# Summing attention scores in three bursts of matmuls a chunk instead of seven

## The chip, the cores and the metric

The kernel runs on one core of a Trainium2 chip. The metric is the device time of one execution in microseconds (us), the median of several runs. The engines are named as in the profile: PE is TensorE (matmuls, with PEld for its weight loads), DVE is VectorE, ACT is ScalarE, POOL is GpSimd, and SP issues most of the transfers.

## The reference

The input is a float32 image batch of 16 x 56 x 56 pixels with 384 channels. Two residual layers are applied:

```python
x = x + attention(group_norm(x))          # layer 0
x = x + binary_depthwise_conv(group_norm(x))   # layer 1, 3x3
```

Layer 0 projects every pixel to a query, a key and a value (384 -> 3 x 384). The channels fall into three groups of 128, which use neighbourhoods of 3 x 3 pixels at distances (dilations) of 1, 2 and 3 pixels. Each group has four heads of 32 channels. For each pixel and head,

```python
score[k] = sum over 32 channels of q[c] * key[c at neighbour k]   # k = 0..8
a = softmax(score / sqrt(32))
out[c] = sum over k of a[k] * value[c at neighbour k]
```

and the result goes through a 384 -> 384 projection with a bias. The change is about the first of these lines: three groups times nine neighbours are 27 "taps", and for each tap four sums over 32 channels are wanted at every pixel.

## The kernel before, in words

An image is cut into seven chunks of eight rows, 448 pixels, so there are 112 chunks. Channels lie on the 128 partitions and pixels along the free dimension. Three plans describe the work on one chunk: `plan_a` turns the input to channels-first and gathers statistics, `plan_b` does attention, `plan_c` does the second layer. Each plan places its pieces at a step and an order within the step with `at(step, order, piece)`. A chunk follows the one before it by nine steps (`STEP = 9`), so work of many chunks is interleaved: in the nine steps in which chunk m forms its scores, the values of earlier chunks are weighed, the keys of a later chunk are projected, and still older chunks are convolved. At the end all pieces are issued by step and order; within a step scores come before convolutions, those before the weighing, queries, key and value projections, output projections, and the turning of inputs and outputs. The framework fixes each engine's instruction order when the kernel is built, near this order but not the same, and gives out the buffers of the pools; on the chip every engine works through its own list.

The score work of a chunk, steps 0 to 8:

- `query(g)` (L435) fills the one PSUM buffer `pq` with the query of group g: six matmul records of L416. It is placed at step -1 + 3g, that is one step before the products of its group.
- `score(i)` (L458), i = 0 to 8, is one row of three taps: one DVE multiplication (L466) of `pq` with three shifted views of the key gives a tile `t` of 128 x 1344. Tiles come from the pool `t_p`.
- `score_round()` (L441) sums taps over the channels of each head. For one tap this is a matmul of the tap's 448 columns with a constant `sel` of 128 x 32 (L451), which adds up four heads and puts them into four of 32 rows of `ps`. Tap p goes to rows 32(p mod 4) onward, so four taps in a row use four different column quarters of PE and can run side by side. Call four such taps a round; 27 taps make seven rounds, the last one of three.
- Every float32 matmul shows as two records, so a full round is 8 MATMUL records.
- Before, a round is issued as soon as four taps are ready: after i = 1, 2, 3, 5, 6, 7 and 8. That makes seven bursts. `in_one_go` keeps a burst together, and puts the newest tap first, so that the one wait for DVE is at the start.
- After the last round `softmax_1` copies `ps` out and the weights are formed.

Other PE work that is named below: `pkv` is the projection of keys and values (L416, 12 records for one key and one value group, at steps 0, 3 and 6), `po` the output projection (L562, 6 records, steps 6, 7 and 8), `pb_a` the spreading of softmax weights over channels (L529, each step), `pc` the second layer's convolution (L656, 24 records, steps 2 and 5, with 32 output columns as in a score round), `pt_x`, `pt_o` and `pt_s` transpositions.

`xr` (pool `xr_p`) holds the residual of a chunk, three tiles of 128 x 448, the same size as one `t`. `load_residual` fetches it, `out_project` adds to it (L565), and after the third part it is stored to `x1d` (L570), which frees it.

Of the kernel before, what the change touches and what calls it, by code (L numbers as in the profile page):

```python
# [20 lines left out]
NG = 3  # L21
NTAP = 9
NQ = 4
# [12 lines left out]
def dilated_attention_then_binary_conv(  # L36
# [186 lines left out]

    dr_p = ctx.enter_context(tc.tile_pool(name="dr_p", bufs=3, space=DRAM))
    xn_p = ctx.enter_context(tc.tile_pool(name="xn_p", bufs=3))
    xr_p = ctx.enter_context(tc.tile_pool(name="xr_p", bufs=2))
    t_p = ctx.enter_context(tc.tile_pool(name="t_p", bufs=3))
    w_p = ctx.enter_context(tc.tile_pool(name="w_p", bufs=3))
    y_p = ctx.enter_context(tc.tile_pool(name="y_p", bufs=4))
    s_p = ctx.enter_context(tc.tile_pool(name="s_p", bufs=1))  # L230
# [30 lines left out]
    def rows(ap):  # L261
        return ap.rearrange("p (r w) -> p r w", w=W)

    def three(t, d, ky):

        tw = t[:, ky * d : ky * d + ROWS, 0:W]
        return bass.AP(tw.tensor, tw.offset, [tw.ap[0], (d, 3), *tw.ap[1:]])

    def in_one_go(matmuls):

        matmuls[0]()
        with tc.high_priority():
            for m in matmuls[1:]:
                tc.keep_in_program_order(m())
# [126 lines left out]
    def plan_b(m, t0):  # L401
# [36 lines left out]

        ready = []

        def score_round():  # L441

            burst = ready[:NQ]
            del ready[:NQ]
            if "ps" not in had:
                had["ps"] = ps_s.tile([P, 512], F32, tag="s", name="ps")

            def add(p, tk):
                j, i = p % NQ, p // NQ
                s0 = SEL0 - 4 * i  # L450
                return nc.tensor.matmul(  # L451
                    had["ps"][32 * j : 32 * j + 32, :PX], sel[:, s0 : s0 + 32], tk,
                    start=(i == 0), stop=(p + NQ >= NG * NTAP),
                )

            in_one_go([lambda a=a: add(*a) for a in burst[-1:] + burst[:-1]])

        def score(i):  # L458

            g, ky = divmod(i, 3)  # L460
            d = DIL[g]
            qg = rows(had["q"][:, :PX])
            q3 = bass.AP(qg.tensor, qg.offset, [qg.ap[0], (0, 3), *qg.ap[1:]])
            k3 = three(kv[0][g][m % K_SLOTS], d, ky)
            t = t_p.tile([P, 3, PX], F32, tag="t", name="t")
            nc.vector.tensor_tensor(t.rearrange("p k (r w) -> p k r w", w=W), q3, k3, ALU.mult)  # L466
            ready.extend((i * 3 + kx, t[:, kx, :]) for kx in range(3))
            if len(ready) >= NQ or i == 8:
                score_round()

        GH = NG * HEADS
        weights = ew.rearrange("p (s v) -> p s v", s=NSUB)[:, :, :NR]
# [121 lines left out]
        for i in range(9):  # L594
            at(t0 + i, SCORE, lambda i=i: score(i))
# [188 lines left out]
```

## Time and profile before

| | before |
|---|---|
| median of 3 runs | 5464.58 us (5464.06 to 5466.99) |
| profiled span | 5462.3 us |
| PE busy | 5293.4 us (97%) |
| POOL busy | 4212.5 us (77%) |
| DVE busy | 4157.7 us (76%) |
| ACT busy | 2412.6 us (44%) |
| score matmuls `ps` L451 | 6048 records, 751.9 us busy |

"Busy" is the time in which an engine has at least one instruction in flight. Matmuls are pipelined, so PE can be busy all the time and still lose time between two kinds of matmul; such losses are read from the starts of consecutive groups in the timeline. A time in the timeline is the start of a group of like instructions, followed by how long the group was in flight.

### The profile page before, as it was taken

How to read it: one execution, taken by the hardware profiler on the slowest of the kernel's cores; microseconds unless marked ns; L12 is line 12 of the kernel's file. 1: busy time of each engine (PE TensorE's matmuls, PEld its weight loads, DVE VectorE, ACT ScalarE, POOL GpSimd, SP SyncE). 2: the span in 40 equal slices, each digit the busy share in tenths (PEclk: the TensorE clock that was granted, in tenths of full speed). 3: DMA queues.
4: the chain of work that ended last, by engine and by line, in shares of the span. 5: the costliest groups of instructions: out<-in, count | busy, mean ns of one | idle time of the engine just before them, and what ended most of it. 6: DMA issues, size and time to landing. Idle time of an engine off the chain costs nothing. (4 is left out here: it accounts for less than half of the span.)

```text
span 5462.3 us, 76025 instructions
## 1 busy us (share of the span) xinstructions
PE 5293.4 (97%) x26901; PEld 2335.4 (43%) x26901; DVE 4157.7 (76%) x4179; ACT 2412.6 (44%) x4203; POOL 4212.5 (77%) x3041
## 2 busy tenths in 40 slices
PE   6999999999999999999999999999999999999956
PEld 4443444444444444444444444444444444444422
DVE  3887778777777777777777778777777777877843
ACT  2223444444444444444444444544444444444433
POOL 1667788788888888888888888888888888888860
PEclk8999999999999999999999999999999999999975
DMA  5433556555555555555555555555555555545435
GB/s 165 131 105 107 153 159 166 159 156 156 157 159 160 158 159 164 155 158 158 160 164 155 160 160 159 162 158 158 155 157 157 161 161 159 160 133 135 129 93 140
DMA packets 833859, 827.88 MB, mean 152 GB/s; under 512 B 381379, under 2 KB 823238, under 8 KB 833478
## 3 DMA queue, kind: packets, MB, share of 16 engines
q1 hardware_dynamic: 825280, 817.58, 55.0%
q10 hardware_dynamic: 8198, 5.43, 0.3%
q8 instruction: 213, 3.49, 0.3%
q14 instruction: 168, 1.38, 0.1%
HBM read 468.47 MB, written 231.21 MB: 128 GB/s over the span
## 5 line engine op out<-in xcount | busy, mean ns | idle before, releaser
L544 POOL TENSOR_TENSOR w<-w 128x1344 f32<-128x1344 f32 x672 | 2049.9, 3050 | 516.2 <-DVE w L536 493.1
L466 DVE TENSOR_TENSOR t<-pq,k 128x1344 f32<-128x1344 f32 x1008 | 1535.6, 1550 | 247.7 <-PE pq L416 244.6
L416 PE MATMUL pkv<-xn,wqkvT 128*128 128x448 f32 x4032 | 1671.1, 554 | 1.3 <-ACT xa L382 1.2
L536 DVE TENSOR_TENSOR w<-pb_a,v 128x1344 f32<-128x1344 f32 x1008 | 1557.3, 1545 | 141.0 <-PE pb_a L529 74.7
L416 PEld LDWEIGHTS pkv<-xn,wqkvT 128*128 128x128 f32 x4032 | 719.9, 190 | 773.6 <-issue 727.5
L562 PE MATMUL po<-y,wprojT 128*128 128x448 f32 x2016 | 839.1, 551 | 36.1 <-POOL y L548 36.1
L416 PE MATMUL pq<-xn,wqkvT 128*128 128x448 f32 x2016 | 852.5, 558 | 0.0
L709 POOL TENSOR_TENSOR m<-m 128x1344 f32<-128x1344 f32 x210 | 639.3, 3044 | 216.0 <-ACT m L703 215.9
L639 ACT ACTIVATE z<-z,mrz 96x448 f32<-96x448 f32 x896 | 617.1, 751 | 361.4 <-DMA z<-x1d 310.9
L451 PE MATMUL ps<-t,sel 128*32 128x448 f32 x6048 | 751.9, 552 | 6.0 <-DVE t L466 6.0
L703 ACT ACTIVATE m<-zg,ktap 128x448 f32<-128x448 f32 x945 | 556.2, 657 | 292.0 <-POOL m L709 287.6
L656 PE MATMUL pc<-z,kdiag 96*32 96x440 f32 (+1 forms) x5376 | 578.5, 565 | 46.1 <-ACT z L639 26.7
L562 PEld LDWEIGHTS po<-y,wprojT 128*128 128x128 f32 x2016 | 375.2, 191 | 398.3 <-issue 345.0
L565 DVE SCALAR_TENSOR_TENSOR xr<-po,bias,xr 128x448 f32<-128x448 f32 x336 | 228.6, 680 | 369.3 <-PE po L562 369.2
L416 PEld LDWEIGHTS pq<-xn,wqkvT 128*128 128x128 f32 x2016 | 355.0, 190 | 328.9 <-issue 328.9
L663 DVE TENSOR_TENSOR x<-pc,x 128x448 f32<-128x448 f32 x224 | 139.8, 624 | 386.9 <-PE pc L656 386.9
L548 POOL TENSOR_TENSOR y<-y,w 128x448 f32<-128x448 f32 x336 | 382.5, 1138 | 23.4
L529 PE MATMUL pb_a<-aT,spread 24*128 24x448 bf16 x3024 | 383.3, 359 | 11.5 <-DVE w L536 11.2
L547 POOL TENSOR_TENSOR y<-w 128x448 f32<-128x448 f32 x336 | 382.3, 1138 | 13.8
L426 ACT COPY v<-pkv 128x448 f32<-128x448 f32 x336 | 179.6, 535 | 446.6 <-PE pkv L416 436.9
L382 ACT COPY xa<-pt_x 128x448 f32<-128x448 f32 x336 | 179.0, 533 | 399.3 <-PE pt_x L378 376.8
L426 ACT COPY k<-pkv 128x448 f32<-128x448 f32 x336 | 179.1, 533 | 391.9 <-PE pkv L416 391.3
(113 smaller groups left out, 4146.8 us busy)
## 6 DMA issues: line engine op xcount, KB each, us to landing
z<-x1d SPq DMA_DIRECT2D x608, 224.0 KB, 4.4
xn<-xd SPq DMA_DIRECT2D x112, 672.0 KB, 4.6
xr<-xd SPq DMA_DIRECT2D x112, 672.0 KB, 4.3
x1d<-xr SPq DMA_DIRECT2D x112, 672.0 KB, 3.2
out_dram<-osb SPq DMA_DIRECT2D x448, 168.0 KB, 2.9
xin<-in_x_dram SPq DMA_DIRECT2D x108, 672.0 KB, 7.0
xd<-xa SPq DMA_DIRECT2D x315, 224.0 KB, 3.1
x<-x1d SPq DMA_DIRECT2D x112, 448.0 KB, 8.2
```

The lines of the kernel that those rows point to most:

```text
L416: nc.tensor.matmul(dst[:, :PX], wqkvT[:, cc, o0 : o0 + P], had["xn"][:, cc, :], start=(cc == 0), stop=(cc == NG - 1))
L451: return nc.tensor.matmul(had["ps"][32 * j : 32 * j + 32, :PX], sel[:, s0 : s0 + 32], tk, start=(i == 0), stop=(p + NQ >= NG * NTAP),)
L466: nc.vector.tensor_tensor(t.rearrange("p k (r w) -> p k r w", w=W), q3, k3, ALU.mult)
L529: return nc.tensor.matmul(pb[:, kx, :PX].rearrange("p (s n) -> p s n", s=NSUB), spread[rows_of, v % 2, :], had["a"][rows_of, :, v // 8, :] ...
L536: nc.vector.tensor_tensor(w.rearrange("p k (r w) -> p k r w", w=W), pb[:, :, :PX].rearrange("p k (r w) -> p k r w", w=W), three(kv[1][g][m ...
L544: nc.gpsimd.tensor_tensor(w0, w0, w, ALU.add)
L548: nc.gpsimd.tensor_tensor(y, y, w0[:, 2], ALU.add)
L562: nc.tensor.matmul(po[:, :PX], wprojT[:, g, j * P : (j + 1) * P], had[f"y{g}"], start=(g == 0), stop=(g == NG - 1))
L639: nc.scalar.activation(z[:, q], z[:, q], AF.Identity, bias=mrz[:, j, q, 0:1], scale=mrz[:, j, q, 1:2])
L656: return nc.tensor.matmul(pcr[q * HD : (q + 1) * HD, :, lo:hi], kdiag[:, kx, j * NQ + q, :], rows(z[:, q])[:, :, lo + kx - 1 : hi + kx - 1 ...
L703: nc.scalar.activation(rows(t[:, kx]), zp[:, ky : ky + ROWS, kx : kx + W], AF.Copy, scale=ktap[:, o : o + 1])
L709: nc.gpsimd.tensor_tensor(had["m"], had["m"], t, ALU.add)
```

## The change

The rounds are gathered into three bursts, after i = 2, 5 and 8, of two, two and three rounds (8, 8 and 11 matmuls). The aim is to have fewer changes between the score matmuls and other PE work. Up to four tiles `t` are alive then: after i = 2 one of nine taps is left over, and after i = 5 two of ten. So `t_p` gets four buffers instead of three, and the memory comes from `xr_p`, which goes from two to one. The flags that start and stop a sum in `ps` are counted by column quarter, since the newest tap of a burst of several rounds is now issued ahead of earlier taps of the same quarter. The number of matmuls, of multiplications and of transfers stays the same.

```diff
-    xr_p = ctx.enter_context(tc.tile_pool(name="xr_p", bufs=2))
-    t_p = ctx.enter_context(tc.tile_pool(name="t_p", bufs=3))
+    xr_p = ctx.enter_context(tc.tile_pool(name="xr_p", bufs=1))
+    t_p = ctx.enter_context(tc.tile_pool(name="t_p", bufs=4))
...
-        def score_round():
-
-            burst = ready[:NQ]
-            del ready[:NQ]
+        issued = [0] * NQ
+
+        def score_rounds(rounds):
+
+            burst = ready[: rounds * NQ]
+            del ready[: rounds * NQ]
...
+                issued[j] += 1
                 return nc.tensor.matmul(
                     had["ps"][32 * j : 32 * j + 32, :PX], sel[:, s0 : s0 + 32], tk,
-                    start=(i == 0), stop=(p + NQ >= NG * NTAP),
+                    start=(issued[j] == 1), stop=(issued[j] == len(range(j, NG * NTAP, NQ))),
                 )
...
-            if len(ready) >= NQ or i == 8:
-                score_round()
+            if i % 3 == 2:
+                score_rounds(3 if i == 8 else 2)
```

## The prediction, made before the changed kernel was run

> **What bounds the kernel now.** I read the page's busy table first, then the table by stage, then PE's timeline over one chunk, and beside it DVE's. The first two say where the bound is:
>
> ```profile
> PE 5293.4 (97%) x26901; PEld 2335.4 (43%) x26901; DVE 4157.7 (76%) x4179; ACT 2412.6 (44%) x4203; POOL 4212.5 (77%) x3041
> ```
>
> ```profile
> 2500.00:3000.00 500.00, 500.00 (x2598) 221.72 (x2597) 394.12 (x395) 234.22 (x410) 409.08 (x287) 1.00 0.58 159
> ```
>
> In the second line (stretch, length, then PE, PEld, DVE, ACT and POOL busy, granted clock, DMA share, GB/s) PE is busy for all 500 us at full clock, and the lines from 600 to 5150 us look alike. POOL has 409 and DVE 394 of 500. The list of PE's waits between 1000 and 5000 us is empty. So the time is PE's: what a chunk costs on PE, times 112, plus the ends. But busy is not useful. PE's timeline over the score steps of one chunk (start, time in flight, records) shows what a burst costs there, if one takes the distance from one start to the next:
>
> ```profile
> 2359.91 4.78 PE L416 MATMUL pkv<-xn,wqkvT 128*128 128x448 f32 x12
> 2364.52 0.55 PE L378 MATMUL pt_x<-ident,xin 112*128 112x112 f32 x4
> ...
> 2365.33 0.96 PE L451 MATMUL ps<-t,sel 128*32 128x448 f32 x8
> 2366.22 0.36 PE L529 MATMUL pb_a<-aT,spread 24*128 24x448 bf16 x3
> ...
> 2366.99 0.96 PE L451 MATMUL ps<-t,sel 128*32 128x448 f32 x8
> 2367.76 2.42 PE L656 MATMUL pc<-z,kdiag 96*32 96x448 f32 x24
> ...
> 2373.87 1.02 PE L416 MATMUL pkv<-xn,wqkvT 128*128 128x448 f32 x2
> 2374.82 0.96 PE L451 MATMUL ps<-t,sel 128*32 128x448 f32 x8
> 2375.70 4.03 PE L416 MATMUL pkv<-xn,wqkvT 128*128 128x448 f32 x10
> 2379.57 0.38 PE L724 MATMUL pt_o<-ident,x 128*112 128x128 f32 x2
> ...
> 2395.03 0.96 PE L451 MATMUL ps<-t,sel 128*32 128x448 f32 x8
> 2395.93 0.36 PE L529 MATMUL pb_a<-aT,spread 24*128 24x448 bf16 x3
> ```
>
> The first two lines are a key and value projection left whole: 4.61 us from its start to the next group. Lower down the same twelve records are cut in two by the burst of i = 3, and from 2373.87 to 2379.57 it is 5.70 us. The burst in the middle of the projection costs 1.09 us. The bursts of i = 1 and 7 stand ahead of a `pb_a` and cost 0.89 and 0.90. The burst of i = 2 stands ahead of the convolution and costs only 0.77. The price of a round depends on its neighbours. The kernel's start has one longer burst, two rounds that met by chance:
>
> ```profile
> 100.70 1.71 PE L451 MATMUL ps<-t,sel 128*32 128x448 f32 x16
> 102.34 1.02 PE L416 MATMUL pq<-xn,wqkvT 128*128 128x448 f32 x2
> ```
>
> Two rounds take 1.64 us there ahead of a 128-column projection, so the second round adds 1.64 - 0.89 = 0.75 us. That is the bare price of a round; all above it (0.34, 0.14, 0.15 and 0.02 in the cases above) is paid for changing over.
>
> **What the Trainium skill says.** TensorEngine Tiling (Array Packing), Key Properties: "Mode switching requires drain". It gives no time for it. The trace agrees: rounds use 128 x 32 tiles, projections 128 x 128, and the changeover is the 0.34 us above; between a round and `pc`, both of 32 columns, there is next to none. TensorE: Matmul & The Clock Gate, Part 3, says that matmuls in different tiles of the array run side by side while matmuls start and end in order; four score matmuls, 8 records, take 0.75 us here, while 6 records of a 128 x 128 projection are about 2.3 us, so the trace agrees. Trainium Kernel Development and Optimization, Best Practices, warns not to take matmul busy time for closeness to the roofline; here PE is 100% busy in the middle while about 1 us a chunk is changeovers.
>
> **The change, part by part.** Where do the three bursts land? In the trace PE's order follows the steps, except that the bursts of i = 3 and i = 6 come later than their place, inside the projection. They follow a fresh query (`pq` at 2370.40 and 2384.23), and their product isn't ready when PE gets to them. The bursts of i = 2, 5 and 8 are not of that kind and stay at their place: i = 2 and 5 directly ahead of the `pc` of their step, i = 8 between an output projection and a `pb_a`.
>
> Removed are the bursts of i = 1, 3, 6 and 7. Those of 3 and 6 cost 1.09 each (for 6: from 2386.98 to 2392.68 is 5.70 against 4.61 again), those of 1 and 7 0.89 and 0.90. Sum 3.97 us a chunk. Added are four rounds in the bursts that stay: one each to i = 2 and 5, two to i = 8, 4 x 0.75 = 3.00 us. Net on PE: 0.97 us; with rounding of the starts I take 0.95. PE's list is the path, so it counts in full wherever PE is full.
>
> How many chunks: 112. The first three have merged bursts already, at least one each. The stage table has PE at 47.17 of 50 us after 5150 and 26.58 of 50 after 5200, so the last two chunks gain nothing; between 400 and 600 us PE idles 12 us in 200, which takes about two more. That leaves 105, so 100 us. In the 14 chunks where group-norm statistics follow the burst of i = 1, its neighbour `pm` has 32 columns too and the burst costs 0.78, so 14 x 0.11 = 1.5 us less. 98.5 us.
>
> What the change adds in waits. Each burst now waits for the third product of its group, and all of it is queued behind that. Bursts 2, 5 and 8 waited for the same products before, so what changes is only that PE reaches them sooner. DVE's timeline of the same chunk:
>
> ```profile
> 2363.96 1.55 DVE L466 TENSOR_TENSOR t<-pq,k 128x1344 f32<-128x1344 f32 x1
> ...
> 2376.43 3.01 DVE L466 TENSOR_TENSOR t<-pq,k 128x1344 f32<-128x1344 f32 x2
> ...
> 2389.73 3.01 DVE L466 TENSOR_TENSOR t<-pq,k 128x1344 f32<-128x1344 f32 x2
> ```
>
> Their ends are 2365.51 (i = 2), 2379.44 (i = 5), 2392.74 (i = 8); the bursts began at 2366.99, 2380.82 and 2398.67, that is 1.48, 1.38 and 5.93 us later. Without the burst of i = 1, burst 2 comes 0.89 sooner: 0.59 left. Without that of i = 3, burst 5 comes 1.09 sooner: 0.29 left. Without 6 and 7, burst 8 has 3.94 left. All stay positive; the least distance from a product to its burst anywhere in the trace is 0.05. I take the wait as zero; the other bound is 0.3 us a burst of i = 2 and 5 if DVE runs half a microsecond later, 0.6 us a chunk.
>
> Four tiles `t`: product n reuses the tile of n - 4. Product 6 follows the query of group 2, which stands behind burst 5 anyway, and product 0 of the next chunk a query behind burst 8; burst 5 and 8 are what frees their tiles. No wait that the query does not impose already. One residual buffer: `load_residual` now comes after the store of the chunk before. In SP's list the store (L570) at 2639.05 is followed by the next load (L552) at 2642.42, which then used the other buffer's release two chunks on; with one buffer the same pair serves adjacent chunks. Store and load take 3.2 and 4.3 us to land by the page, and from the third `xr` operation of a chunk (2359.53) to the first of the next (2395.14) are 35 us. Hidden by at least 25 us. What is queued on SP behind a load that waits is a halo copy and a store, held by 3 us at most, which is what the list shows before as well. Products, exponentials and POOL's sums are the same.
>
> Sum: 5464.6 - 98.5 = 5366 us.
>
> **Rivals.**
> A: the bursts of i = 2 and 5 are late at their place and are put after other work, inside a projection. The small 0.29 and 0.59 us speak for it; against it stands that the convolution, 2.35 us of ready work with the same 32 columns, is next in order and fills such a gap for nothing. Then two bursts cost 0.32 more each, the gain falls to 0.95 - 0.64 = 0.31 us a chunk, 33 us: 5432 us. A milder form (one burst) gives 5399.
> B: PE waits for DVE at the bursts. At 0.6 us a chunk the gain is 0.35, 37 us, 5428. To lose, each of the three must wait 0.5 us, 1.5 a chunk: 0.55 x 112 = 62 us, 5526, slower. Against: DVE is at 79% and idle ahead of each group's first product (0.6 to 0.8 us, waiting for `pq`).
> C: another engine holds the period. Against: in the table POOL, the fullest, has 409 of 500, so it would bind only at 0.82 of the present period. The gain would be nil, 5464.
> D: the one residual buffer holds up SP's list, and with it the halo copies that products need. Were 1.5 us a chunk lost, net 0.55 x 112: again about 5526, slower. The 25 us of room speak against it.
>
> **How the numbers follow.** Forecast 0.76, A 0.09, B with a gain 0.03, B with a loss 0.05, C 0.04, D 0.03. Faster 0.88, same 0.04, slower 0.08. The least time is that of full gain in all 112 chunks at 0.97, 109 us: 5356, and 5350 leaves something for better packing. The upper end takes in A and the mild B: 5434.
>
> **What would show it.** Right: three score bursts a chunk with 16, 16 and 22 records, all projections of twelve records whole at 4.6 us, bursts of 16 at 1.53 us ahead of `pc`, 2.4 us for the 22, the period of a plain chunk (45.8 us now) down to 44.9, and PE still at 500 of 500. Wrong: waits of PE for `t` in the middle of the run, bursts of 16 inside `pkv`, or idle time of PE behind `xr`.

## The result, and the profile after

The changed kernel takes 5443.4 us (median of 6 runs, 5440.4 to 5447.0) against 5464.4 us: the ratio is 0.996, with an interval of 0.9947 to 0.9973. That is 21 us faster. The forecast was 98.5 us faster, 5366 us, with a range of 5350 to 5434, and the measured time lies above the range.

The bursts do what was forecast. PE's timeline of the changed kernel (start, time in flight, records):

```profile
2200.76 2.46 PE L454 MATMUL ps<-t,sel 128*32 128x448 f32 x22
2203.15 0.36 PE L532 MATMUL pb_a<-aT,spread 24*128 24x448 bf16 x3
...
2215.86 1.71 PE L454 MATMUL ps<-t,sel 128*32 128x448 f32 x16
2217.39 2.41 PE L659 MATMUL pc<-z,kdiag 96*32 96x448 f32 x24
...
2224.16 4.78 PE L416 MATMUL pkv<-xn,wqkvT 128*128 128x448 f32 x12
2228.78 0.38 PE L727 MATMUL pt_o<-ident,x 128*112 128x128 f32 x2
```

From start to start: 2.39 us for the burst of 22 records, 1.53 for one of 16 ahead of `pc`, 4.62 for the projection, which is whole again. From one group of `pt_s` to the next, a plain chunk has gone from 45.8 to 44.9 us. But the table by stage no longer shows a full PE:

```profile
2500.00:3000.00 500.00, 496.42 (x2592) 231.74 (x2594) 397.83 (x397) 238.98 (x416) 412.28 (x286) 0.99 0.59 160
```

(The same stretch, with the same columns, had 500.00 and a clock of 1.00 before.) Of PE's waits between 600 and 5000 us, us in total, times and the longest, the first is a new one:

```profile
PE pp L335 <- POOL pair L330: 41.1, 13, 3.2
PE po L565 <- ACT k L426: 4.3, 5, 1.5
PE pt_s L489 <- ACT sT L486: 3.4, 2, 1.7
PE ps L454 <- DVE t L469: 2.7, 6, 0.9
```

The waits that the prediction worried about, a burst for its product, are the last line, 2.7 us. The first line has 13 waits in 13 images of the stretch. `pp` is the last PE step of the group norm of layer 1 (`spread_out`): three small matmuls that spread mean and deviation, the tile `pair`, over channels. GpSimd makes `pair` in `invert` with thirteen small operations: three Newton steps of an inverse square root, four operations each, and a product. PE's timeline around one of the thirteen:

```profile
2090.73 2.52 PE L416 MATMUL pq<-xn,wqkvT 128*128 128x448 f32 x6
2096.41 0.80 PE L335 MATMUL pp<-pair,gselT 32*128 32x2 f32 x3 [3.16 <-POOL pair L330]
...
2098.17 6.84 PE L416 MATMUL pkv<-xn,wqkvT 128*128 128x448 f32 x12
2104.85 1.67 PE L565 MATMUL po<-y,wprojT 128*128 128x448 f32 x4
```

Two losses follow one another. PE stands idle for 3.16 us, and then the same projection that took 4.62 takes 6.68 us. The table of short stretches (the eighth column group is the granted clock, ahead of the DMA share and GB/s) says why:

```profile
2090.50:2093.50 3.00, 2.75 (x10) 1.08 (x9) 2.30 (x3) 0.00 (x0) 2.84 (x7) 1.00 0.89 237
2093.50:2096.40 2.90, 0.00 (x0) 0.00 (x0) 1.35 (x1) 0.00 (x0) 2.28 (x11) 0.85 1.02 199
2096.40:2099.00 2.60, 2.59 (x10) 1.88 (x11) 0.81 (x2) 0.88 (x2) 0.00 (x0) 0.50 0.13 27
2099.00:2102.00 3.00, 3.00 (x5) 1.35 (x4) 3.00 (x3) 0.60 (x1) 2.00 (x1) 0.50 0.07 1
2102.00:2105.00 3.00, 3.00 (x9) 1.63 (x8) 0.84 (x1) 2.21 (x4) 1.03 (x1) 0.94 0.09 1
```

During the idle time, in other images up to 2 us after it, the clock is halved. The trace's clock records have 13 such stretches between 600 and 5000 us, one per image, of 3.4 or 6.8 us, 64.9 us together; the kernel before has none there. PE is busy for 60.9 of the 64.9 us (the rest is idle time, counted already), and as work at half clock takes twice as long, half of that is lost, 30.4 us. The chunk with these statistics takes 51.9 to 53.5 us instead of 47.8. Together 41.1 + 30.4 = 71.5 us of the 77.5 that are missing.

Why is `pair` late? GpSimd's timeline, first before, then after:

```profile
2098.80 3.05 POOL L544 TENSOR_TENSOR w<-w 128x1344 f32<-128x1344 f32 x1 [1.79 <-DVE w L536]
2103.16 0.18 POOL L326 TENSOR_TENSOR var<-var 32x1 f32<-32x1 f32 x1 [1.31 <-DVE var L319]
...
2106.34 0.18 POOL L330 TENSOR_TENSOR pair<-pair 32x1 f32<-32x1 f32 x1
2106.48 3.02 POOL L544 TENSOR_TENSOR w<-w 128x1344 f32<-128x1344 f32 x1
```

```profile
2087.92 3.05 POOL L547 TENSOR_TENSOR w<-w 128x1344 f32<-128x1344 f32 x1 [1.74 <-DVE var L319]
2090.92 0.18 POOL L326 TENSOR_TENSOR var<-var 32x1 f32<-32x1 f32 x1
2091.19 0.19 POOL L327 TENSOR_TENSOR var<-var 32x1 f32<-32x1 f32 x1
2091.33 1.13 POOL L550 TENSOR_TENSOR y<-w 128x448 f32<-128x448 f32 x1
...
2092.85 1.12 POOL L551 TENSOR_TENSOR y<-y,w 128x448 f32<-128x448 f32 x1
...
2096.17 0.18 POOL L330 TENSOR_TENSOR pair<-pair 32x1 f32<-32x1 f32 x1
```

Before, the chain comes first and the 3 us sum of `w` after it. After, that sum is ahead of the chain and two sums `y` of 1.13 us are inside it. The number of operations is the same; their order in GpSimd's list, fixed when the kernel was built, is another. The order on DVE has turned too. Its timeline, before and after (L315, L318 and L319 are the three operations that turn `pv` into the tile `var`):

```profile
2102.58 0.14 DVE L315 TENSOR_SCALAR var<-pv 32x1 f32<-32x1 f32 x1 [0.94 <-PE pv L312]
...
2102.94 0.14 DVE L319 TENSOR_SCALAR var<-var 32x1 int32<-32x1 int32 x1
2103.05 1.56 DVE L536 TENSOR_TENSOR w<-pb_a,v 128x1344 f32<-128x1344 f32 x1
```

```profile
2082.98 3.01 DVE L469 TENSOR_TENSOR t<-pq,k 128x1344 f32<-128x1344 f32 x2
2085.91 0.14 DVE L315 TENSOR_SCALAR var<-pv 32x1 f32<-32x1 f32 x1
2086.08 0.14 DVE L318 TENSOR_SCALAR var<-var 32x1 int32<-32x1 int32 x1
2086.22 1.56 DVE L539 TENSOR_TENSOR w<-pb_a,v 128x1344 f32<-128x1344 f32 x1
2087.69 0.13 DVE L319 TENSOR_SCALAR var<-var 32x1 int32<-32x1 int32 x1
```

Before, DVE waits 0.94 us for `pv` and does all three variance operations ahead of the product `w`; after, it doesn't wait, and the 1.56 us product stands between the second and the third. PE's own steps around this, before and then after (the end of the part after is shown above):

```profile
2102.20 0.35 PE L312 MATMUL pv<-dev,gsel 128*32 128x1 f32 x6
...
2106.72 2.52 PE L416 MATMUL pq<-xn,wqkvT 128*128 128x448 f32 x6
2109.17 0.49 PE L335 MATMUL pp<-pair,gselT 32*128 32x2 f32 x3
```

```profile
2085.45 0.35 PE L312 MATMUL pv<-dev,gsel 128*32 128x1 f32 x6
```

From the start of `pv` the pair is ready after 4.3 us before and after 10.9 us in the changed kernel, in all 13 images. The 6.6 us between the two are 1.5 for the product on DVE, 3.0 for the sum ahead of the chain, and 2.1 for what stands inside it. Without a wait PE would come to `pp` 7.7 us after `pv` (2.45 us after the start of `pq`, as before), against 7.0 before, because the burst of i = 5 in between is longer by a round. So 2.65 us to spare, plus 0.76, less 6.57, is the wait of 3.16 us.

Why did the order turn? Counted from the query ahead of them, the variance matmuls `pv` come 1.09 us sooner than before (8.50 us against 9.59), because the burst of i = 3 no longer stands in the projection in between. That this lead made the build choose another order is inferred; a trace does not show how the build chooses.

### The profile page after: what moved, and what is told of

It is laid out like the page before. It is cut to its first block, busy times and chain, and to the rows that moved or that the text cites. A ratio compares the mean times of both kernels' runs of the same rounds, so it can differ in the third digit from the quotient of the medians.

```text
span 5442.3 us, 75958 instructions
## 1 busy us (share of the span) xinstructions
PE 5218.2 (96%) x26901; PEld 2414.7 (44%) x26901; DVE 4153.8 (76%) x4179; ACT 2417.9 (44%) x4203; POOL 4213.6 (77%) x3041
## 5 line engine op out<-in xcount | busy, mean ns | idle before, releaser
L416 PE MATMUL pkv<-xn,wqkvT 128*128 128x448 f32 x4032 | 1636.3, 556 | 0.2 <-ACT xn L412 0.2
L416 PEld LDWEIGHTS pkv<-xn,wqkvT 128*128 128x128 f32 x4032 | 749.7, 193 | 704.2 <-issue 674.8
L454 PE MATMUL ps<-t,sel 128*32 128x448 f32 x6048 | 661.2, 547 | 13.2 <-DVE t L469 11.5
L659 PEld LDWEIGHTS pc<-z,kdiag 96*32 96x32 f32 x5376 | 176.2, 114 | 386.0 <-issue 329.5
```

Source lines behind the costliest of these rows:

```text
L416: nc.tensor.matmul(dst[:, :PX], wqkvT[:, cc, o0 : o0 + P], had["xn"][:, cc, :], start=(cc == 0), stop=(cc == NG - 1))
L454: return nc.tensor.matmul(had["ps"][32 * j : 32 * j + 32, :PX], sel[:, s0 : s0 + 32], tk, start=(issued[j] == 1), stop=(issued[j] == len(r ...
L659: return nc.tensor.matmul(pcr[q * HD : (q + 1) * HD, :, lo:hi], kdiag[:, kx, j * NQ + q, :], rows(z[:, q])[:, :, lo + kx - 1 : hi + kx - 1 ...
```

## The experiments

My theory: PE's lead of 1.09 us at `pv` turns the order on DVE and GpSimd, `pair` comes late, PE idles and then runs at half clock. Rivals: the bursts' own waits, the single residual buffer, or a clock that drops for another reason.

**The buffers alone.** The kernel before, with `t_p` at four and `xr_p` at one:

```diff
-    xr_p = ctx.enter_context(tc.tile_pool(name="xr_p", bufs=2))
-    t_p = ctx.enter_context(tc.tile_pool(name="t_p", bufs=3))
+    xr_p = ctx.enter_context(tc.tile_pool(name="xr_p", bufs=1))
+    t_p = ctx.enter_context(tc.tile_pool(name="t_p", bufs=4))
```

> The kernel before with the buffers of the change alone: four tiles t, one xr, still seven bursts. Main theory: the buffers take no part, 5464 us within 5. Rival (the single residual buffer holds up transfers once per image): slower by up to the 85 us that the changed kernel lacks, 5480 to 5550 us.

Measured: 5467.1 us, ratio 1.0004 (0.9995 to 1.0013). By themselves the buffers take no part that can be measured.

**One round split off again.** The changed kernel with the burst of i = 3 back:

```diff
-            if i % 3 == 2:
-                score_rounds(3 if i == 8 else 2)
+            if i in (2, 3, 5, 8):
+                score_rounds({2: 2, 3: 1, 5: 1, 8: 3}[i])
```

> The changed kernel with one round split off again: bursts after i = 2, 3, 5 and 8 of 2, 1, 1 and 3 rounds. The burst of i = 3 cuts a projection once more and costs 0.34 us a chunk, about 36 us. Main theory: it also delays PE by 1.09 us ahead of the variance matmuls pv, so that DVE and GpSimd keep the order of the kernel before (the chain of 13 small operations ahead of the 3 us sum) and the wait at pp is gone: 5358 + 36 = 5394 us, faster than the changed kernel although it has a dearer burst. Rival (the loss does not hang on PE's lead there): 5443 + 36 = 5479 us.

Measured: 5406.5 us, ratio 0.9891 (0.9876 to 0.9906). A kernel with a dearer set of bursts is 37 us faster than the changed one. The wait at `pp` is not among PE's waits between 600 and 5000 us any more, and in GpSimd's list the chain stands ahead of the sum again. The pair is ready 4.3 us after `pv`, as before. 12 us remain over the expected 5394; in the profiled run, of 5411.1 us, PE idles for 12.4 us between 600 and 5000 us and loses 4.8 to half clock. The largest wait left is

```profile
PE po L565 <- ACT k L426: 8.7, 10, 2.7
```

**The chain one step earlier.** `STAT1_SLICE` gives the steps of the six statistics pieces of layer 1: channel sums, mean, deviation, variance, inversion and spreading. The changed kernel, with two of them, variance and inversion, moved:

```diff
-    STAT1_SLICE = (0, 1, 2, 4, 4, 6)
+    STAT1_SLICE = (0, 1, 2, 3, 3, 6)
```

> The changed kernel, with the variance and inversion pieces of the second group norm placed one step earlier (slices 3 and 3 instead of 4 and 4); pp stays at its place. Main theory: GpSimd gets the chain of 13 small operations ahead of the long sum, the pair is ready before PE reaches pp: 5358 us, between 5350 and 5375, as for the run with pp later. Rival (bursts or buffers): 5443 us.

Measured: 5387.8 us, ratio 0.9858 (0.9844 to 0.9873). The bursts are untouched and 56 us come back: the pair is now ready 4.3 us before PE comes to `pp`. It misses the 5350 to 5375 that I had given. In PE's waits, `pp` is replaced by a smaller wait one link further up:

```profile
PE pv L312 <- POOL dev L306: 14.0, 13, 1.8
```

**`pp` one step later.** The changed kernel, with the last piece at slice 7:

```diff
-    STAT1_SLICE = (0, 1, 2, 4, 4, 6)
+    STAT1_SLICE = (0, 1, 2, 4, 4, 7)
```

> The changed kernel, with one edit: the last statistics piece of the second group norm (the matmuls pp that spread mean and deviation over channels) is placed one step later, at slice 7 instead of 6. Main theory (once per image PE reaches pp before GpSimd has finished the pair, waits some 3.2 us and then runs at half clock for 3.4 to 6.8 us): a step is over 7 us of PE work, so the wait is gone, no half clock in the middle of the run, 85 us come back: 5358 us, between 5350 and 5372. Rival (the loss lies in the bursts' own waits for DVE, or in the single residual buffer): no change, 5443 us.

Measured: 5451.6 us, ratio 0.9977 (0.9967 to 0.9987). A miss: the wait at `pp` is gone, and another of nearly the same size has come, with half clock behind it.

```profile
PE pt_o L727 <- ACT v L426: 40.7, 13, 3.1
PE pt_o L727 <- ACT k L426: 10.0, 13, 0.9
```

ACT's timeline of that run, in which a bracket is idle time and what ended it, shows what PE waited for:

```profile
2108.55 1.79 ACT L706 ACTIVATE m<-zg,ktap 128x448 f32<-128x448 f32 x3 [5.21 <-POOL m L712]
2110.24 5.31 ACT L642 ACTIVATE z<-z,mrz 96x448 f32<-96x448 f32 x8
...
2116.56 0.51 ACT L426 COPY v<-pkv 128x448 f32<-128x448 f32 x1
```

ACT needs the spread mean and deviation for the convolution's input. That work, on which GpSimd's sums `m` wait, and the copies of `pkv` stand in one list on ACT. When `pp` comes a step later, ACT waits 5.21 us for a buffer `m`, and the copy that frees the next PSUM buffer for PE stands behind that. So the statistics have a deadline on ACT as well, and it isn't past `pp`'s old place. The run says nothing against the theory of the wait, but it does against my view that PE was the only one to wait for it.

**One and two Newton steps.** The changed kernel with a shorter chain in GpSimd, at the same places. It leaves out two of the three steps (in a second run one of them), so the norms are less exact; the edit for one step is:

```diff
-            for step in range(3):
+            for step in range(1):
...
-                nc.gpsimd.tensor_tensor(pair[:, 1:2] if step == 2 else r, r, t, ALU.mult)
+                nc.gpsimd.tensor_tensor(pair[:, 1:2] if step == 0 else r, r, t, ALU.mult)
```

> The changed kernel with one Newton step of the inverse square root instead of three (two of three steps of that computation are left out, so the norms are less exact); order and places are the same otherwise. GpSimd's chain ahead of the pair is 8 operations shorter, 8 x 0.265 = 2.1 us of the 3.2 us by which it was late. Main theory: the wait at pp falls to about 1.1 us an image and the clock no longer drops: 5388 us within 15, about 55 us faster than the changed kernel, more than the 14 x 2.1 = 29 us that the shorter wait alone gives. Rival (only the wait counts, the half clock has another cause): 5443 - 29 = 5414 us with the clock still at half once per image.

> The changed kernel with two Newton steps instead of three (one of three steps of the inverse square root is left out). The chain is 4 operations shorter, 1.06 us, so PE should wait about 2.1 us at pp instead of 3.2 (one step: 0.94 measured, with no half clock). If half clock follows only an idle time near that of the changed kernel, the clock stays full in the middle of the run and the time is that of the one-step run plus 14 x 1.1: 5392 us within 8. If any idle time over 2 us halves the clock, it is 13 to 23 us more: 5405 to 5415.

Measured: 5377.0 us with one step, ratio 0.9838 (0.9824 to 0.9853); 5410.2 us with two, ratio 0.9901 (0.9886 to 0.9916). The first line of PE's waits, with one step and with two:

```profile
PE pp L335 <- POOL pair L330: 12.2, 13, 1.2
```

```profile
PE pp L335 <- POOL pair L330: 25.7, 13, 2.0
```

| Newton steps | mean wait of PE at `pp` | images with half clock there | time |
|---|---|---|---|
| 3 (the change) | 3.16 us | 13 of 13 | 5443.4 us |
| 2 | 1.98 us | 6 of 13 | 5410.2 us |
| 1 | 0.94 us | 0 of 13 | 5377.0 us |

The wait falls by about the length of the operations left out (four times 0.265 us a step), and half clock goes with it. From three steps to one, 66 us come back: 28.9 from the wait and 30.4 from the clock make 59.

**A longer chain in the kernel before**, with eight Newton steps; bursts and buffers untouched:

```diff
-            for step in range(3):
+            for step in range(8):
...
-                nc.gpsimd.tensor_tensor(pair[:, 1:2] if step == 2 else r, r, t, ALU.mult)
+                nc.gpsimd.tensor_tensor(pair[:, 1:2] if step == 7 else r, r, t, ALU.mult)
```

> The kernel before (seven bursts, old buffers) with eight Newton steps instead of three: 20 operations of 0.265 us more on GpSimd ahead of the pair, 5.3 us, and two sums y of 1.14 us fall in between; PE had 2.65 us to spare at pp. Main theory: PE waits about 4.9 us at pp once per image and then has half clock for 3.4 to 6.8 us: 7 to 8 us in each of 14 images, 5556 to 5580 us, with bursts and buffers untouched. Rival 1 (a wait at pp does not bring half clock): 5464 + 69 = 5533 us. Rival 2 (the statistics do not hold PE; the loss belongs to the merged bursts): 5464 us.

Measured: 5709.9 us, ratio 1.0449 (1.0432 to 1.0467). The direction holds, the size was far too small.

```profile
PE pp L335 <- POOL pair L330: 131.7, 26, 7.6
```

There are 26 waits, not 13: the group norm of layer 0 uses the same chain, and I had counted only that of layer 1. The clock records show 208.2 us at half clock in the same stretch, in 26 pieces. Part of that, 62.4 us, is idle time too, and must not be counted twice. Over the whole span PE idles 166.2 us more than in the kernel before and loses 83.8 us more to half clock, together 250 us for a time that is 246 us longer. The loss needs neither merged bursts nor new buffers.

**`dev` on VectorE.** The run with the chain one step earlier, and these two lines changed:

```diff
-            nc.gpsimd.tensor_tensor(dev, dev, dev, ALU.mult)
-            nc.gpsimd.tensor_tensor(dev, dev, ch[:, :, 1], ALU.add)
+            nc.vector.tensor_tensor(dev, dev, dev, ALU.mult)
+            nc.vector.tensor_tensor(dev, dev, ch[:, :, 1], ALU.add)
```

> The run with the chain one step earlier, and in addition the two small operations on dev are on VectorE instead of GpSimd, where they stood behind a 1.13 us sum; in that run PE waited 1.1 us in each of 13 images for them at pv, 14.0 us in all. Main theory: 5388 - 14 = 5374 us, within 8 us of the 5366 that were forecast for the change. Rival (the rest of the gap to 5366 is elsewhere): 5388 us.

Measured: 5406.8 us, ratio 0.9894 (0.9879 to 0.9909), 19 us slower than without that edit and a miss of the 5374 expected. The wait at `pv` for GpSimd is gone, but DVE is later elsewhere:

```profile
PE pb_a L532 <- DVE w L539: 15.4, 15, 1.1
PE ps L454 <- DVE t L469: 8.3, 19, 1.5
```

Which of these orders did it is not shown.

**Three pieces one step earlier.** The changed kernel, with the deviation moved as well:

```diff
-    STAT1_SLICE = (0, 1, 2, 4, 4, 6)
+    STAT1_SLICE = (0, 1, 1, 3, 3, 6)
```

> The changed kernel with three pieces of the second group norm one step earlier: deviation at slice 1 instead of 2, variance and inversion at 3 instead of 4. Against the run with only the last two moved, the small operations on dev come ahead of both sums y on GpSimd, so the 1.1 us wait at pv (14.0 us in 13 images) should go: 5374 us within 8, near the forecast of 5366. If a new wait takes its place, as with dev on VectorE: 5388 us or more.

Measured: 5374.8 us, ratio 0.9836 (0.9819 to 0.9852). This computes all that the kernels before and after compute and is faster than both, by 89 us and 69 us. The table by stage has PE full again in the stretch shown above:

```profile
2500.00:3000.00 500.00, 499.97 (x2636) 232.11 (x2629) 401.20 (x398) 238.92 (x417) 416.44 (x289) 1.00 0.59 161
```

**All runs in one account.** From each trace one can take PE's idle time (nothing in flight) and the time lost to half clock (half of the time in which PE was busy at half clock). What is left of the span is PE's own work at full clock, in us:

| kernel | span | PE idle | lost to half clock | left |
|---|---|---|---|---|
| before, seven bursts | 5462.3 | 168.9 | 76.6 | 5216.8 |
| before, long chain | 5708.0 | 335.1 | 160.4 | 5212.5 |
| changed, burst of i = 3 back | 5409.4 | 177.7 | 79.6 | 5152.1 |
| changed, three bursts | 5442.3 | 224.1 | 106.5 | 5111.7 |
| changed, three pieces earlier | 5380.6 | 179.9 | 88.4 | 5112.3 |

The buffers alone leave 5215.4, and the other five runs with three bursts 5112.1 to 5115.7. So what is left depends on the bursts alone, to within about 4 us. The change took 105.1 us off PE's work, and 55.2 us more idle time and 29.9 us more lost clock took back 85.1 of them.

## Why the prediction was wrong

What it said on PE's own work was right: where the three bursts land, 16, 16 and 22 records, 1.53 and 2.39 us each, whole projections, 45.8 to 44.9 us for a plain chunk. By the account above this work fell by 105.1 us, where 98.5 were forecast. With the statistics out of the way most of the gain is there: 5374.8 against the 5366 forecast. Rivals A and D did not happen, and the mild form of B is 2.7 us of waits in all. The room of the residual buffer was as large as stated.

The step that failed is the sentence "what changes is only that PE reaches them sooner", with the earlier one, "PE's list is the path, so it counts in full wherever PE is full". I checked what the bursts, the tiles and the transfers wait for, and nothing else. Each of the four removed bursts moves all later PE work of its chunk ahead against the other engines, and I gave two bursts' margins of that lead (0.59 and 0.29 us) but not those of the other PE instructions that wait for another engine. The nearest was in the trace of before: the pair was ready at 2106.52 and `pp` started at 2109.17, 2.65 us to spare, of which a single displaced sum of 3.05 us takes all. I also took the order on DVE and GpSimd as given, and that is what failed in the end. The lead itself moved `pv` and `pp` together, and by PE's own steps the 2.65 us would have grown to 3.4; the new order made the pair 6.57 us later and PE wait 3.16 us in each image. With the burst of i = 3 put back, the old order is back as well. No run changes the lead and nothing else, so that the lead turned the order stays an inference.

The second thing missing was the price of a wait. I priced idle time on PE at its own length. Here 41.1 us of waits brought 64.9 us at half clock, which cost 30.4 us more. The Trainium skill has this (TensorE: Matmul & The Clock Gate, Why this matters for your kernels): no idle gaps over about 3 us between bursts, or the clock is halved. The trace agrees for waits of 3.16 us, in 13 images of 13; but waits of 1.98 us already did it in 6 of 13, so the figure is no safe limit here.

In the section on the rivals, C had the right form, another engine holding PE, but I judged it by GpSimd's mean load, 409 of 500 us. It held PE once per image, in a stretch where its load in order, not its mean, counted.

The last 9 us between 5374.8 and 5366 fit into the waits that are left: in the profiled run, of 5382.4 us, PE idles for 12.6 us between 600 and 5000 us and loses 6.5 to half clock. What stays open is how the build came to the other order, and why VectorE takes the two small operations so badly.

## What to carry to other kernels

When work is taken off the busiest engine, list every instruction on it that waits for another engine, with its slack in the trace of before, and not only those that the edit touches. Then compare the other engines' lists before and after: here PE's lead alone would have cost nothing at `pp`, but orders fixed at build time turned and took 6.6 us, more than twice the slack. Work that comes once per image on a chain through four engines has no weight in the busy table and can still take most of a gain that is made in every chunk. Where such a chain is late, move its start earlier before its end later: the engine behind it had a deadline too.

## What the runs showed of the hardware

Idle times of PE and the clock after them: waits of 0.9 to 1.2 us at `pp` were followed by half clock in none of 13 images (one Newton step), waits of 1.98 us in 6 of 13 (two steps), waits of 2.55 us in 13 of 13 (layer 0, long chain) and waits of 3.16 us in 13 of 13 (the change). The length alone does not settle it: single waits of 1.22 to 1.26 us were followed by half clock in three other runs (the burst of i = 3 back, the chain one step earlier, the three pieces earlier), and two of 1.65 and 1.73 us in the changed kernel were not. In every trace the half-clock stretches start whole multiples of 3.41 us apart (those at 798.48 and 1122.74 us in the changed kernel, for one, 95 times 3.4133), and all but the last of each trace, which the kernel's end cuts off, last whole multiples of it: 3.4 or 6.8 us after the waits at `pp` in the changed kernel, 10.2 us after the waits of 7.6 us of the long chain. So it may matter where a wait falls on this grid of 3.41 us; no run here tests that. A wait just over 3 us cost PE about 5.5 us an image: 3.2 us idle and 2.3 us of lost clock.
